# Top-32 selection from pair and quad maxima, and no filler products, in a gated cross-attention and expert block

## The chip, the cores and the metric

One core of one Trainium2 chip runs the whole program as one launch. The metric is device time in microseconds (us). Six runs of the kernel before lie between 1881.35 and 1894.25 us, with a median of 1891.92 us. The engines are named as in the profile: PE multiplies matrices, DVE, ACT and POOL work elementwise, SP issues most transfers. PE writes its products to PSUM, which has eight banks of 512 fp32 values in each of 128 partitions; the other tiles lie in SBUF.

## The reference, cut to what matters

Eight batches of 512 tokens by 256 features pass through two gated blocks. The first is a cross-attention that keeps, in each row of scores, only the 32 largest of 1024, and drives a FiLM modulation around a long convolution, followed by an MLP. The second is a mixture of experts with one of eight experts for each token, beside a shared one. The change is in the attention's selection:

```python
Q = (x_text @ Wq).reshape(Bb, Tt, H, DH)          # 8 x 512 tokens, 4 heads of 32
K = (x_vision @ Wk).reshape(Bb, Gg, H, DH)        # 1024 context rows
scores = jnp.einsum('bthd,bghd->bhtg', Q, K) / np.sqrt(DH)
topv, topi = jax.lax.top_k(scores, K_TOP)         # 32 of 1024 in each row
probs = jax.nn.softmax(topv, axis=-1)
attn = jnp.zeros_like(scores).at[bi, hi, ti, topi].set(probs)
attn_mean = attn.mean(axis=1)                     # over the 4 heads
V = x_vision @ Wv
c_t = jnp.einsum('btg,bgd->btd', attn_mean, V)
```

## The kernel before

**An order by a plan.** The kernel doesn't issue its operations as it writes them. `Plan.note` records each with an engine, an estimated cost and its dependencies, read off the tiles that it reads and writes (lines 100 to 218). `Plan.order` (220 to 307) then plays the program through on those estimates: of the operations that are ready it takes the one that can begin first, and among equals the one with the lowest place `k`; it also grants the buffers of each pool. The result is one fixed order for each engine, and every engine works through its own in order. `Plan.issue` (318 to 326) issues them, so nearly every instruction of the profile bears line 326 and has to be told by its tiles.

**The fillers.** The plan notes how long PE would be idle before each operation (`o.idle`, line 284). Ahead of each PE operation, `issue` calls `busy` (1407), which issues products of `ones16` with itself, 512 columns wide, into a PSUM bank `idle` of its own: one for each 0.22 us of 85% of that idle time, of which at most 12 us are counted (lines 325 and 332). Nobody reads `idle`. In the built program it is 1525 products.

**PSUM.** Its eight banks are two for scores (`ps_sc`), two for accumulators (`ps_ac`), three for all other products (`ps_mm`) and one for the fillers (`ps_id`), lines 389 to 392.

**The work.** Four streams are recorded beside each other: `prepare` (437) loads a batch and makes `kT` and `qT`; `attention` (910) goes through 8 batches x 4 token tiles x 2 pairs of heads, which is 64 pairs; behind it, a batch later, `mixed` (1058) and `after_mix` (1100) do the convolution, the MLP and the shared expert; `routed` (1336) runs 38 blocks of 128 tokens through their expert. Beside the first batch, `setup` (610) makes the convolution's kernel. The last batch's remaining work and 19 of the blocks make a tail without attention, from about 1592 us of the span on.

**One pair of heads** (lines 935 to 986). `scores` has PE make two heads' rows of scores for 128 tokens (`pS`), a pair ahead, and ACT copies them to `sc` (128 x 1024). Then, for each head:

- DVE takes the maximum of the scores' two halves, `mn[:, 0]`, 512 wide (line 943). POOL makes the minimum beside it, exactly, by integers: it adds the halves' bits and subtracts those of the maximum, `mn[:, 1]` (945, 946).
- DVE scans the 512 maxima for the 32 largest: MAX8 gives eight, MATCH_REPLACE strikes them out into `left`, four and three times (948 to 956).
- ACT computes the exponentials `e`, with the largest score subtracted (958).
- DVE scans the 512 minima for their eight largest (965); eight of these and the last eight of the first scan give the row's threshold `th` (967 to 969).
- DVE multiplies `e` by `sc >= th` and sums it (977); ACT counts by signs (979), scales by the sum (982), and POOL adds the heads up in `acc` (984). When a token tile is done, `weighted` (875) transposes `acc` and multiplies it with the context on PE.

The tiles `mn`, `left`, `e`, `top` and `acc` have two buffers each, so those of the next pair wait for this pair's last readers.

**The guard.** At the end the counts must say that exactly 32 scores passed in every row; if not, a general branch computes everything anew (1415 to 1447). The selection above is exact as long as no more than eight of a row's 32 largest are the smaller one of their two halves.

Of the kernel before, what the change touches and what calls it, by code (L numbers as in the profile page):

```python
# [12 lines left out]
F32 = mybir.dt.float32  # L13
# [3 lines left out]
I32 = mybir.dt.int32  # L17
AF = mybir.ActivationFunctionType
ALU = mybir.AluOpType
AX = mybir.AxisListType  # L20
PSUM = bass.MemoryType.PSUM

P = 128
# [20 lines left out]


class Op:
    __slots__ = ("i", "eng", "fn", "cost", "lat", "table", "acc", "succ", "npred", "est", "tiles", "end", "start", "what", "k", "idle")


class Plan:  # L50
# [169 lines left out]
    def order(self):  # L220

        ops = self.ops
        free = {e: 0.0 for e in ("PE", "DVE", "ACT", "POOL", "SP")}
        table = None
        wire = 0.0
        left = {t: len(v[1]) for t, v in self.tiles.items()}
        last = {t: 0.0 for t in self.tiles}
        slots = {}
        for q in self.queues.values():
            slots[id(q)] = [0.0] * q[0]  # L230
        granted = set()
        avail = {e: [] for e in free}
        done = []

        def offer(op):
            op.npred -= 1
            if op.npred == 0:
                avail[op.eng].append(op)

        for op in ops:  # L240
            op.npred += 1 + len(op.tiles)

        def grant(q):
            s = slots[id(q)]
            while s and q[2] < len(q[1]):
                t = q[1][q[2]]
                q[2] += 1
                at = min(s)
                s.remove(at)
                for i in self.tiles[t][1]:  # L250
                    ops[i].est = max(ops[i].est, at)
                    offer(ops[i])

        for q in self.queues.values():
            grant(q)
        for op in ops:
            offer(op)
        total = len(ops)
        while len(done) < total:
            best = None  # L260
            for e, a in avail.items():
                if not a:
                    continue
                t = free[e]
                first = min(max(t, o.est) for o in a)
                c = None
                for o in a:
                    if o.est <= first:
                        k = o.k + (SWITCH if e == "ACT" and o.table not in (None, table) else 0)
                        if c is None or k < c[0]:  # L270
                            c = (k, o)
                o = c[1]
                st = max(t, o.est)
                if best is None or (st, o.k) < best[0]:
                    best = ((st, o.k), o, st)
            assert best is not None, "nothing can begin"
            _, o, st = best
            e = o.eng
            avail[e].remove(o)
            cost = o.cost  # L280
            if e == "ACT" and o.table not in (None, table):
                cost += 1.3
                table = o.table
            o.start, o.idle = st, st - free[e]
            free[e] = o.end = st + cost
            done.append(o)
            if o.lat is not None:
                wire = max(o.end, wire) + (o.lat - 2.9 if o.lat > 2.9 else 0.0)
                fin = max(o.end + o.lat, wire + 2.9)
                o.end = fin  # L290
            else:
                fin = o.end
            for i in o.succ:
                s = ops[i]
                hop = HOP["DMA" if o.lat is not None else e] if (s.eng != e or o.lat is not None) else 0.0
                s.est = max(s.est, fin + hop)
                offer(s)
            for t in o.tiles:
                left[t] -= 1
                last[t] = max(last[t], fin)  # L300
                if left[t] == 0:
                    q = self.tiles[t][0]
                    slots[id(q)].append(last[t] + 0.15)
                    grant(q)
        self.total = max(o.end for o in ops)
        self.free = free
        return done
# [7 lines left out]
                return  # L315
            yield

    def issue(self, tc, busy):

        self.noting = False  # L320
        ET = mybir.EngineType
        with tc.manual_schedule(engines={ET.PE, ET.DVE, ET.Activation, ET.Pool, ET.SP}):
            for o in self.order():
                if o.eng == "PE":
                    busy(int(min(o.idle, FILL_MAX) * FILL / STEP))
                o.fn()  # L326


SLOW = 1.05


FILL_MAX, FILL, STEP = 12.0, 0.85, 0.22
SWITCH = 100
WIRE = 350e3
NPREP = 13
# [5 lines left out]
def bc(ap, axis, n):  # L341

    ap = ap.unsqueeze(axis)
    shape = list(ap.shape)
    shape[axis] = n
    return ap.broadcast_to(shape)
# [3 lines left out]
def tile_kernel(ctx: ExitStack, tc: tile.TileContext, a: dict, out: bass.AP):  # L350
    nc = tc.nc
    x, cx = a["x"], a["ctx_768"]
    B, T, D = x.shape
    G, DV = cx.shape[1:]
    H, DH = 4, 32
    KTOP = 32
    HID = a["L0_xattn_W1"].shape[1]
    NST = a["L0_xattn_A_re"].shape[1]
    NE, _, NI = a["L0_ffn_rt_gate"].shape
# [4 lines left out]

    L = T // 2
    NL, NFFT = L // P, 2 * L
    SCALE = 1.0 / float(np.sqrt(np.float32(DH)))


# [15 lines left out]
    pk = ctx.enter_context(tc.tile_pool(name="pk", bufs=2))  # L385
# [2 lines left out]
    dr = ctx.enter_context(tc.tile_pool(name="dr", bufs=1, space=bass.MemoryType.DRAM))  # L388
    ps_sc = ctx.enter_context(tc.tile_pool(name="ps_sc", bufs=1, space=PSUM))
    ps_ac = ctx.enter_context(tc.tile_pool(name="ps_ac", bufs=2, space=PSUM))  # L390
    ps_mm = ctx.enter_context(tc.tile_pool(name="ps_mm", bufs=3, space=PSUM))
    ps_id = ctx.enter_context(tc.tile_pool(name="ps_id", bufs=1, space=PSUM))
    ctx.enter_context(nc.allow_non_contiguous_dma(reason="small vectors"))

    plan = Plan(nc)
    V, S, GP, TE, SY = (plan.engine(n, e) for n, e in (
        ("DVE", nc.vector), ("ACT", nc.scalar), ("POOL", nc.gpsimd), ("PE", nc.tensor), ("SP", nc.sync)))
# [4 lines left out]
    def bank(name, pool=ps_mm, tag="mm"):  # L402
        return pool.tile([P, 512], F32, tag=tag, name=name)
# [13 lines left out]
    ones16 = const.tile([P, P], BF16, name="ones16")  # L417
# [136 lines left out]
    free = const.tile([P, NE], I32, name="free")  # L554
# [355 lines left out]
    def attention(states):  # L910
# [5 lines left out]
        for k, (b, t, h0) in enumerate(steps):  # L916
            s, sc = states[b], ahead
# [10 lines left out]
            if h0 == 0:  # L928
                acc = pk.tile([P, G], F32, tag="acc", name=f"acc{b}_{t}")
            n = f"{b}_{t}_{h0}"  # L930
# [4 lines left out]
            top = pk.tile([P, 2, KTOP + 8], F32, tag="top", name="top" + n)  # L935
            sm = pk.tile([P, 5, 2], F32, tag="sm", name="sm" + n)
            nm, nb, na, su, ri = (sm[:, k_, :] for k_ in range(5))
            e_, mn = [], []
            for i in range(2):
                m_ = pk.tile([P, 2, G // 2], F32, tag="mn", name=f"mn{n}_{i}")  # L940
                mn.append(m_)
                lo, hi = sc[i][:, : G // 2], sc[i][:, G // 2 :]
                V.tensor_tensor(m_[:, 0], lo, hi, ALU.max)
                mi = m_.bitcast(I32)
                GP.tensor_tensor(mi[:, 1], lo.bitcast(I32), hi.bitcast(I32), ALU.add)
                GP.tensor_tensor(mi[:, 1], mi[:, 1], mi[:, 0], ALU.subtract)
            for i in range(2):
                for r in range(KTOP // 8):
                    t8 = top[:, i, r * 8 : r * 8 + 8]
                    src = mn[i][:, 0] if r == 0 else left  # L950
                    V.max(t8, src)
                    if r == 0:
                        S.activation(nm[:, i : i + 1], t8[:, 0:1], AF.Copy, scale=-SCALE)
                        left = pk.tile([P, G // 2], F32, tag="left", name=f"left{n}_{i}")
                    if r < KTOP // 8 - 1:
                        V.match_replace(left, t8, src, TAKEN)
                e_.append(pk.tile([P, G], F32, tag="e", name=f"e{n}_{i}"))
                S.activation(e_[i], sc[i], AF.Exp, bias=nm[:, i : i + 1], scale=SCALE)
                if i == 0:
                    yield  # L960
                    if behind is not None:
                        behind()
                        behind = None
            for i in range(2):
                V.max(top[:, i, KTOP:], mn[i][:, 1])
            t8 = pk.tile([P, 2, 8], F32, tag="t8", name="t8" + n)
            for i in range(2):
                V.max(t8[:, i, :], top[:, i, KTOP - 8 :])
# [21 lines left out]
    def attention_masked(b, s):  # L990
# [3 lines left out]
        for t in range(NT):  # L994
            acc = pk.tile([P, G], F32, tag="acc", name=f"acc{b}_{t}")
            for h in range(H):
# [14 lines left out]
                for r in range(KTOP // 8):  # L1011
                    src = sc if r == 0 else wk_
                    V.max(top[:, r * 8 : r * 8 + 8], src)
                    if r == 0:
                        GP.tensor_scalar(sm[:, 0:1], top[:, 0:1], -SCALE, None, ALU.mult)
                    V.match_replace(wk_, top[:, r * 8 : r * 8 + 8], src, TAKEN)
# [385 lines left out]
    together(behind(B - 1))  # L1402
    together((routed(B - 1, 0, TAKE[B - 1]), 1))

    idle = bank("idle", ps_id, "id")

    def busy(n):
        for _ in range(n):
            nc.tensor.matmul(idle, ones16, bc(ones16, 1, 4), start=True, stop=True)  # L1409

    plan.issue(tc, busy)


    ok = const.tile([P, 4], F32, name="ok")
# [74 lines left out]
```

## Time and profile before

| | us | share of the span |
|---|---|---|
| median of six runs | 1891.92 | |
| the profiled execution, as timed | 1875.7 | |
| its span, first to last instruction | 1874.0 | 100% |
| PE busy, fillers included | 1712.3 | 91% |
| of it fillers (1525) | 380.7 | 20% |
| DVE busy | 1465.5 | 78% |
| ACT busy | 1173.8 | 63% |
| POOL busy | 1087.4 | 58% |
| mean granted PE clock | 0.955 of full speed | |

Shares of the whole span mix stages with different limits: the first 281 us hold the setup, from 93 to 1592 us most of the attention and the other streams run beside each other, and after 1592 us DVE is busy for 62 of 188 us and PE for 180. Matmuls are pipelined and their ends are modelled: a filler has a mean of 392 ns in the profile, but the next one starts 216 ns after it at full clock. The granted clock is either 1.00 or 0.50 at any moment, and a stretch of time shows the mean.

### The profile page before, as it was taken

Reading aid. Unit: us, or ns where it says so; the run is one execution under the profiler, and the core shown is the slowest. Engines: PE = TensorE matmul, PEld = TensorE weight load, DVE = VectorE, ACT = ScalarE, POOL = GpSimd, SP = SyncE. Lnnn points to the kernel's source line nnn. Section 1 sums busy time; section 2 is a strip of 40 time slices with the busy share of each in tenths; the row PEclk is TensorE's granted clock in tenths of the full one; section 3 lists DMA queues with packets and bytes.
Section 4 is the critical chain, followed back from the end, with each engine's and each line's share of the span. In section 5 each row is a group of like instructions: output and inputs, shape, how many; then the busy total and the mean of one; then the engine's idle time right before and its main releaser. Section 6 shows DMA issues by size and latency. Waiting matters only on the chain. (4 is left out here: it accounts for less than half of the span.)

```text
span 1874.0 us, 24133 instructions
## 1 busy us (share of the span) xinstructions
PE 1712.3 (91%) x7888; PEld 992.3 (53%) x7888; DVE 1465.5 (78%) x2841; ACT 1173.8 (63%) x2020; POOL 1087.4 (58%) x1048
## 2 busy tenths in 40 slices
PE   8598997999989988999889889998999999899996
PEld 4254543445544544565347444654466546547685
DVE  5999988998889888989778989788998999531210
ACT  6577744577757764797468756976697678413221
POOL 6454435665765666577655856585758676532122
PEclk9799998999999988999989999998999999999998
DMA  4000010001100120044003320233013405532594
GB/s 113 0 1 23 21 46 17 1 12 57 57 17 21 48 62 17 23 135 125 18 12 118 99 70 12 73 114 101 12 53 103 115 1 152 169 115 77 191 286 127
DMA packets 101301, 131.88 MB, mean 70 GB/s; under 512 B 9687, under 2 KB 73004, under 8 KB 101166
## 3 DMA queue, kind: packets, MB, share of 16 engines
q1 hardware_dynamic: 93102, 121.05, 20.5%
q0 software_dynamic: 7008, 8.42, 2.6%
q8 instruction: 64, 1.05, 0.2%
q10 hardware_dynamic: 1056, 0.79, 0.1%
q14 instruction: 71, 0.58, 0.1%
HBM read 112.22 MB, written 18.78 MB: 70 GB/s over the span
## 5 line engine op out<-in xcount | busy, mean ns | idle before, releaser
L1409 PE MATMUL idle<-ones 128*128 128x512 bf16 x1525 | 380.7, 392 | 0.0
L326 POOL TENSOR_TENSOR acc<-acc,e 128x1024 f32<-128x1024 f32 x96 | 232.9, 2426 | 136.3 <-ACT e L326 133.6
L326 POOL TENSOR_TENSOR mn<-sc 128x512 int32<-128x512 int32 x128 | 203.9, 1602 | 154.7 <-DVE top L326 97.1
L326 DVE MAX8 top<-left 128x8 f32<-128x512 f32 x384 | 265.4, 691 | 10.4
L1409 PEld LDWEIGHTS <-ones 128*128 128x128 bf16 x1525 | 148.9, 101 | 197.6 <-issue 64.4
L326 DVE SCALAR_TENSOR_TENSOR e<-sc,t,e 128x1024 f32<-128x1024 f32 x128 | 210.1, 1659 | 18.3 <-ACT e L326 18.3
L326 PE MATMUL pS<-kT,qT 32*128 32x512 f32 x512 | 209.9, 664 | 13.8 <-ACT sc L326 13.3
L326 POOL TENSOR_TENSOR mn<-mn 128x512 int32<-128x512 int32 x128 | 180.7, 1423 | 64.8 <-DVE mn L326 61.5
L326 ACT COPY sc<-pS 128x512 f32<-128x512 f32 x256 | 142.8, 584 | 85.0 <-PE pS L326 65.8
L326 DVE MATCH_REPLACE8 left<-top,left 128x512 f32<-128x512 f32 x256 | 172.9, 675 | 0.0
L326 ACT ACT_TABLE_LOAD x130 | 166.8, 1283 | 7.8 <-PE p L326 2.1
L326 DVE MAX8 top<-mn 128x8 f32<-128x512 f32 x256 | 169.1, 678 | 3.0 <-POOL mn L326 2.7
L326 DVE TENSOR_TENSOR mn<-sc 128x512 f32<-128x512 f32 x128 | 149.9, 1195 | 24.1 <-ACT sc L326 24.1
L326 ACT ACTIVATE e<-sc,sm 128x1024 f32<-128x1024 f32 x128 | 146.1, 1148 | 30.6 <-POOL acc L326 27.1
L326 ACT ACTIVATE junk<-sc,sm 128x1024 bf16<-128x1024 f32 x128 | 146.3, 1143 | 1.3
L326 PE MATMUL pu<-aT,cx 128*96 128x128 f32 x1024 | 131.2, 277 | 0.9 <-ACT aT L326 0.9
L326 PEld LDWEIGHTS pu<-aT,cx 128*96 128x96 f32 x1024 | 119.6, 165 | 21.9 <-issue 15.2
L326 POOL DMA_INDIRECT out_dram<-yb,to x38 | 65.8, 1731 | 106.2 <-DMA out_dram<-yb,to 46.0
L326 PE MATMUL pm<-hT,w 128*128 128x512 f32 x256 | 119.1, 598 | 0.3
L326 PE MATMUL am<-w,ga 128*128 128x256 f32 x512 | 117.5, 380 | 2.0 <-ACT ga L326 2.0
L326 ACT ACTIVATE e<-e,sm 128x1024 f32<-128x1024 f32 x96 | 108.7, 1151 | 3.8 <-DVE sm L326 3.7
L326 DVE TENSOR_TENSOR ger<-sgr,pu 128x512 f32<-128x512 f32 x38 | 26.0, 683 | 106.8 <-PE pu L326 92.3
(288 smaller groups left out, 3194.4 us busy)
## 6 DMA issues: line engine op xcount, KB each, us to landing
rt_gate<-in_L_ffn_rt_gate_dram SPq DMA_DIRECT2D x38, 512.0 KB
rt_up<-in_L_ffn_rt_up_dram SPq DMA_DIRECT2D x38, 512.0 KB
rt_down<-in_L_ffn_rt_down_dram SPq DMA_DIRECT2D x38, 512.0 KB
w<-in_L_xattn_W_dram SPq DMA_DIRECT2D x32, 512.0 KB
cx<-in_ctx_dram SPq DMA_DIRECT2D x7, 768.0 KB
xtab<-zt SPq DMA_DIRECT2D x8, 642.5 KB
xb<-xtab SPq DMA_DIRECT2D x38, 128.5 KB
xt<-in_x_dram SPq DMA_DIRECT2D x8, 512.0 KB
```

What stands on the lines that cost most here:

```text
L326: o.fn()
L1409: nc.tensor.matmul(idle, ones16, bc(ones16, 1, 4), start=True, stop=True)
```

## The change

The halves are halved again. With `Q` = 256, DVE takes, after the maximum of halves, the maximum of that maximum's own halves, `hi`, 256 wide, so each element of `hi` is the largest of four scores. The four MAX8 and three MATCH_REPLACE go over these 256. POOL makes the smaller ones for both levels: as before the 512 of the first (add and subtract), and then the 256 of the second (another add and subtract). Both lie side by side in `mn[:, Q:]`, and one scan over the 768 gives their eight largest. The place of the maxima's first quarter, `mn[:, :Q]`, is where the struck-out rows are now written, and the tag `left` holds `hi`. The rest of a pair is as before. The selection is exact as long as no more than eight of a row's 32 largest are not the largest of their four.

The fillers are gone, with the plan's note of idle time and the bank `idle`, and `ps_mm` has four banks.

```diff
     def issue(self, tc, busy):
...
             for o in self.order():
-                if o.eng == "PE":
-                    busy(int(min(o.idle, FILL_MAX) * FILL / STEP))
                 o.fn()
...
-FILL_MAX, FILL, STEP = 12.0, 0.85, 0.22
...
+    Q = G // 4
...
-    ps_mm = ctx.enter_context(tc.tile_pool(name="ps_mm", bufs=3, space=PSUM))
-    ps_id = ctx.enter_context(tc.tile_pool(name="ps_id", bufs=1, space=PSUM))
+    ps_mm = ctx.enter_context(tc.tile_pool(name="ps_mm", bufs=4, space=PSUM))
...
-            e_, mn = [], []
+            e_, mn, hi = [], [], []
             for i in range(2):
-                m_ = pk.tile([P, 2, G // 2], F32, tag="mn", name=f"mn{n}_{i}")
+                m_ = pk.tile([P, G], F32, tag="mn", name=f"mn{n}_{i}")
                 mn.append(m_)
-                lo, hi = sc[i][:, : G // 2], sc[i][:, G // 2 :]
-                V.tensor_tensor(m_[:, 0], lo, hi, ALU.max)
-                mi = m_.bitcast(I32)
-                GP.tensor_tensor(mi[:, 1], lo.bitcast(I32), hi.bitcast(I32), ALU.add)
-                GP.tensor_tensor(mi[:, 1], mi[:, 1], mi[:, 0], ALU.subtract)
+                V.tensor_tensor(m_[:, : 2 * Q], sc[i][:, : 2 * Q], sc[i][:, 2 * Q :], ALU.max)
             for i in range(2):
+                m_ = mn[i]
+                hi.append(pk.tile([P, Q], F32, tag="left", name=f"hi{n}_{i}"))
+                V.tensor_tensor(hi[i], m_[:, :Q], m_[:, Q : 2 * Q], ALU.max)
+                mi, si = m_.bitcast(I32), sc[i].bitcast(I32)
+                GP.tensor_tensor(mi[:, 2 * Q :], si[:, : 2 * Q], si[:, 2 * Q :], ALU.add)
+                GP.tensor_tensor(mi[:, 2 * Q :], mi[:, 2 * Q :], mi[:, : 2 * Q], ALU.subtract)
+                GP.tensor_tensor(mi[:, Q : 2 * Q], mi[:, :Q], mi[:, Q : 2 * Q], ALU.add)
+                GP.tensor_tensor(mi[:, Q : 2 * Q], mi[:, Q : 2 * Q], hi[i].bitcast(I32), ALU.subtract)
+            for i in range(2):
+                left = mn[i][:, :Q]
                 for r in range(KTOP // 8):
                     t8 = top[:, i, r * 8 : r * 8 + 8]
-                    src = mn[i][:, 0] if r == 0 else left
+                    src = hi[i] if r == 0 else left
                     V.max(t8, src)
...
-                        left = pk.tile([P, G // 2], F32, tag="left", name=f"left{n}_{i}")
                     if r < KTOP // 8 - 1:
                         V.match_replace(left, t8, src, TAKEN)
...
             for i in range(2):
-                V.max(top[:, i, KTOP:], mn[i][:, 1])
+                V.max(top[:, i, KTOP:], mn[i][:, Q:])
...
-    idle = bank("idle", ps_id, "id")
-
-    def busy(n):
-        for _ in range(n):
-            nc.tensor.matmul(idle, ones16, bc(ones16, 1, 4), start=True, stop=True)
-
-    plan.issue(tc, busy)
+    plan.issue(tc)
```

More of the change, by code (lines that the diff above doesn't have):

```diff
@@ L46 @@
 class Op:
-    __slots__ = ("i", "eng", "fn", "cost", "lat", "table", "acc", "succ", "npred", "est", "tiles", "end", "start", "what", "k", "idle")
+    __slots__ = ("i", "eng", "fn", "cost", "lat", "table", "acc", "succ", "npred", "est", "tiles", "end", "start", "what", "k")
 class Plan:
@@ L283, in order @@
                 table = o.table
-            o.start, o.idle = st, st - free[e]
+            o.start = st
             free[e] = o.end = st + cost
@@ L316, in ahead, with issue @@
             yield
-    def issue(self, tc, busy):
+    def issue(self, tc):
         self.noting = False
```

## The prediction

> **What bounds the kernel now.** I read the busy times first, then the same by stage, then the groups, then the waits. The stages, in us of the span (columns: stage, length, then busy time and count of PE, PEld, DVE, ACT, POOL, then granted clock, DMA share, GB/s):
>
> ```profile
> 0.00:93.00 93.00, 63.59 (x252) 28.74 (x252) 70.17 (x127) 54.16 (x102) 48.23 (x68) 0.87 0.22 57
> 93.00:281.00 188.00, 177.53 (x1216) 91.67 (x1217) 175.70 (x255) 129.03 (x205) 88.74 (x58) 0.97 0.07 23
> 281.00:562.00 281.00, 255.81 (x998) 129.20 (x997) 245.93 (x481) 176.98 (x311) 180.37 (x146) 0.96 0.09 27
> 562.00:937.00 375.00, 351.30 (x1403) 194.46 (x1405) 324.98 (x657) 263.16 (x457) 246.76 (x244) 0.95 0.19 56
> 937.00:1311.00 374.00, 341.23 (x1465) 202.18 (x1464) 315.39 (x624) 264.68 (x454) 240.09 (x235) 0.94 0.26 75
> 1311.00:1592.00 281.00, 268.26 (x1196) 161.72 (x1194) 261.90 (x526) 214.21 (x362) 196.89 (x188) 0.98 0.25 72
> 1592.00:1780.00 188.00, 180.15 (x833) 117.65 (x832) 62.36 (x164) 54.62 (x97) 62.00 (x88) 0.98 0.42 138
> ```
>
> From 93 to 1592 us, while the 64 pairs of heads are selected, DVE is busy 175.70 + 245.93 + 324.98 + 315.39 + 261.90 = 1323.9 of 1499 us, 88%; POOL 952.9 us, 64%. PE looks busier, but its fillers are in that number. So DVE paces the selection with 175 us idle, and PE paces the tail after 1592 us. The groups that the change touches (busy us, mean ns of one, idle before):
>
> ```profile
> L1409 PE MATMUL idle<-ones 128*128 128x512 bf16 x1525 | 380.7, 392 | 0.0
> L326 DVE MAX8 top<-left 128x8 f32<-128x512 f32 x384 | 265.4, 691 | 10.4
> L326 DVE SCALAR_TENSOR_TENSOR e<-sc,t,e 128x1024 f32<-128x1024 f32 x128 | 210.1, 1659 | 18.3 <-ACT e L326 18.3
> L326 DVE MAX8 top<-mn 128x8 f32<-128x512 f32 x256 | 169.1, 678 | 3.0 <-POOL mn L326 2.7
> L326 DVE TENSOR_TENSOR mn<-sc 128x512 f32<-128x512 f32 x128 | 149.9, 1195 | 24.1 <-ACT sc L326 24.1
> L326 POOL TENSOR_TENSOR yf<-yf,t 128x256 f32<-128x256 f32 x32 | 27.5, 880 | 0.0
> L326 DVE TENSOR_TENSOR ger<-sgr,pu 128x512 f32<-128x512 f32 x38 | 26.0, 683 | 106.8 <-PE pu L326 92.3 <-PE pxb L326 12.6 <-ACT sgr L326 2.0
> L326 DVE TENSOR_TENSOR xr<-xr,pfo 128x256 f32<-128x256 f32 x64 | 25.8, 418 | 12.5 <-ACT xr L326 4.1 <-DMA xtab<-zt 3.8 <-PE pfo L326 2.1
> L326 DVE MAX8 t<-top 128x8 f32<-128x16 f32 x128 | 18.6, 167 | 0.1
> ```
>
> See the two 512-wide TENSOR_TENSORs: 1195 ns with both operands in SBUF, 683 with one in PSUM. One by one in the trace, the first kind takes about 689 ns in 71 of 128 cases and 1839 on average in the other 57, and those lie almost wholly beside a POOL operation: the two engines hold each other up. Last, three waits (us in total, times, longest):
>
> ```profile
> POOL acc L326 <- ACT e L326: 133.6, 29, 10.3
> POOL mn L326 <- DVE top L326: 97.1, 27, 14.5
> DVE xm L326 <- PE pfi L326: 54.9, 20, 8.6
> ```
>
> POOL is often ahead and waits. In before nobody needs its minima before the last scan.
>
> **The shorter scans.** MAX8 costs (678 - 167) / (512 - 16) = 1.03 ns an element, so 256 elements save 0.264 us. Per head, four MAX8 and three MATCH_REPLACE (675 ns at 512; same slope taken) shrink: 7 x 0.264 = 1.85 us; the scan of the rest grows from 512 to 768: 0.264 back. Over 128 heads: -203 us.
>
> **The added maximum of quarters (DVE, 256 wide, two SBUF operands).** Before has 418 ns for this size with one operand in PSUM; the held-up half-maximum is 0.51 over its PSUM twin. I take 0.93 us x 128 = +119 us; bounds 0.418 (54 us) and 0.418 plus one whole 512-wide POOL operation, 1.27 (216 us). I take the middle because POOL is by construction at work on the same pair just then.
>
> **More holding up.** The half-maximum loses 0.51, the 1024-wide selection 1659 - 1219 (its PSUM neighbour) = 0.44: 122 us over 128 heads. POOL gets 2 x 0.87 us per head more (the 880 ns row): 223 us, so 64% becomes some 78% and the 122 us grow by 23%: +28 us. Bounds 0 and 60. DVE net: -203 + 119 + 28 = **-56 us**. POOL's 223 us themselves lie beside DVE and are not added.
>
> **The new wait.** The first MATCH_REPLACE of a head now writes into the first quarter of `mn`, which POOL must have read: its 512-wide add and subtract and the 256-wide add come first. Behind it in DVE's queue stand the scans of both heads, the thresholds, and with them ACT's and POOL's work of the pair. In the timeline of the 64 pairs POOL's subtract of the first head ends 5.60 us on average (median 4.53, one in ten over 11.35) after DVE began the pair; plus 0.87 is 6.5. DVE's own work until then: two half-maxima, two quarter-maxima, two MAX8: 2 x (1.195 + 0.93 + 0.41) = 5.1. That is 1.4 us short. The built order of the changed program, priced with these rows, says the same: between the two points POOL has 9.6 us queued on average, other operations included, DVE 8.1. So some 1.45 x 64 = 93 us; I count two thirds, **+60 us**, since part falls on the 175 us that DVE idles anyway. Bounds: 0 (POOL begins early, as it often could) and 192 (only the pairs where POOL is late, 3.0 us a pair).
>
> **The fillers go.** Of their runs, those followed at once by a real product may have held it up: 86 us before 281 us, 90 from there to 1592, 22 after. Against that stands the clock:
>
> ```profile
> 516.00:519.20 3.20, 1.13 (x11) 0.91 (x9) 3.10 (x6) 0.37 (x1) 0.00 (x0) 1.00 0.16 32
> 519.20:522.60 3.40, 0.62 (x3) 0.63 (x4) 2.69 (x6) 0.00 (x0) 3.06 (x2) 0.51 0.61 201
> ```
>
> PE was busy for a third of a step, and the next step ran at half clock, where the filler's spacing is 427 ns for 216. Cutting the record of the clock into its 3.41 us steps, all 19 full-clock steps with PE under 47% busy are followed by a half-clock one, and a drop lasts 1.7 steps on average. With the fillers struck out of the trace, low steps between 281 and 1592 us rise from 20 to 64: 44 x 1.7 x 3.41 / 2 = 128 us of PE time lost, against 90 at most won. A third of either counts, since DVE paces this stage and PE ends under two thirds of its idle time: 43 - 30 = **+13 us** (bounds -90, +128). In the tail PE is the path: 5 more low steps, +14, less 22: **-8**. At the start the products before the first selection at 32 us sum to some 7 us at full clock; **+5** of it (0 to 10). Between 32 and 281 us DVE covers PE, so 86 us won and 50 low steps count nothing; without that cover it is within those bounds.
>
> The Trainium skill, in TensorE: Matmul & The Clock Gate, "What's actually happening", puts the return to half clock after an idle window of about 3.4 us. The trace is stricter: the step above was a third busy. Wholly idle steps in that stage would rise from 3 to 22, so by the rule the 128 us would be an estimated 55, the share on the path 18 and the sum 25 us lower.
>
> **The fourth bank.** PE's list of waits shows none that a product bank ends; 0, bounds -20 and +10. DMA work is the same, except in place.
>
> **Sum:** -56 + 60 + 13 - 8 + 5 = +14 us. The profiled execution took 1875.7 us (span 1874.0), so 1890; the six runs have their median at 1891.92, 0.87% above, and the forecast at that level is **1906 us**.
>
> **Rivals.**
> (1) *POOL keeps ahead*, and the new wait vanishes. It decides if the first 256-wide add ends within 5.1 us of the pair's start in most pairs; half of the subtracts end within 4.53 already, which speaks for it, the acc waits of up to 10.3 us in POOL's queue against. Then -56 + 10 = -46, and with the quarter-maximum at its floor -111: 1765 to 1830 and, at the median's level, 1780 to 1846. The faster side, with what lies between it and my forecast.
> (2) *The clock bounds it*: PE has so little to spare after 562 us that all 128 us and none of the 90 count. It decides once real products fill most half-clock steps. +14 - 13 + 128 = +129: 2005, at the median's level 2022.
> (3) *POOL bounds it*: per pair its work becomes (952.9 + 223) / 64 = 18.4 us, and if it keeps before's idle 547 / 64 = 8.5, a pair takes 26.9 instead of 23.4: +224 us, some 2115; half of that is likelier.
> (4) *The selection fails its own test*, and the general branch runs: that needs a row with over 8 of its 32 largest outside the quarter-maxima. Counted from the given inputs, the worst of 16,384 rows has 7. Under 1%.
>
> **How the numbers follow.** Within 1886 to 1950, the forecast's terms as taken or somewhat worse: 0.42 (0.09 of it within 0.3% of before, which is about what a measurement can tell from no change; 0.33 slower). Rival 1 and what lies between: 0.36. Rivals 2 and 3, in whole or half: 0.22. So faster 0.36, same 0.09, slower 0.55. Both signs hold much, so the forecast's own range is 1886 to 1950, and the one for 8 in 10 is 1815 to 2015.
>
> **What would show it.** DVE's MAX8 at 256 near 0.41 us; the 256-wide maximum near 0.9; a new group of waits of DVE's first MATCH_REPLACE on POOL `mn` near 60 to 90 us; the clock near 0.85 instead of 0.955; DVE's busy time near 1410. Wrong if that wait stays under 20 us, or if DVE idles on PE's products instead.

## The result, and the profile after

The changed kernel takes 1891.69 us (median of 35 runs, 1884.53 to 1894.54), the kernel before 1883.16 us (median of 77): a ratio of **1.0038, 95% interval 1.0024 to 1.0051**. It is slower by 7.2 us of 1883. The six runs that the forecast was read against had their median 0.5% above that of the 77. Of the twelve runs of experiment e2 below, three (1893 to 1897 us, at a clock of 0.83) count as slow and are left out of its ratio; with them its mean ratio would be 0.9989, so every size below that rests on e2 could be some 7 us off. The profiled execution has a span of 1889.2 us against 1874.0.

The same stages as before (stage, length, busy time and count of PE, PEld, DVE, ACT, POOL, clock, DMA share, GB/s):

```profile
93.00:281.00 188.00, 105.57 (x729) 64.90 (x729) 167.28 (x257) 127.35 (x199) 108.03 (x75) 0.61 0.07 22
281.00:562.00 281.00, 219.41 (x681) 114.39 (x682) 221.06 (x481) 166.00 (x296) 209.62 (x188) 0.78 0.08 27
562.00:937.00 375.00, 327.01 (x1204) 185.25 (x1203) 306.56 (x679) 262.45 (x456) 296.32 (x301) 0.87 0.18 56
937.00:1311.00 374.00, 327.82 (x1342) 197.65 (x1341) 302.98 (x683) 269.57 (x467) 294.26 (x308) 0.90 0.25 75
1311.00:1592.00 281.00, 257.10 (x980) 148.62 (x978) 234.97 (x535) 194.91 (x335) 227.72 (x222) 0.89 0.19 57
1592.00:1780.00 188.00, 162.52 (x705) 108.05 (x703) 69.53 (x191) 70.43 (x120) 82.16 (x108) 0.93 0.43 143
```

From 93 to 1592 us DVE's busy time fell from 1323.9 to 1232.9 us and POOL's rose from 952.9 to 1136.0. Yet the last maximum of halves begins at 1598.5 us, where it began at 1588.2: DVE has 91 us less to do in that stretch (78.5 us less in the whole span) and is no sooner done. The clock fell in every stage, to a mean of 0.837. The groups (busy us, mean ns, idle before):

```profile
L323 DVE SCALAR_TENSOR_TENSOR e<-sc,t,e 128x1024 f32<-128x1024 f32 x128 | 204.4, 1612 | 18.1 <-ACT e L323 16.7
...
L323 DVE MAX8 top<-mn 128x8 f32<-128x256 f32 x384 | 163.9, 427 | 12.2
...
L323 DVE TENSOR_TENSOR mn<-sc 128x512 f32<-128x512 f32 x128 | 138.8, 1107 | 7.0 <-ACT sc L323 6.9
L323 DVE TENSOR_TENSOR hi<-mn 128x256 f32<-128x256 f32 x128 | 133.0, 1065 | 0.6
...
L323 DVE MAX8 top<-mn 128x8 f32<-128x768 f32 x128 | 119.2, 944 | 7.0 <-POOL mn L323 6.9
L323 POOL TENSOR_TENSOR mn<-mn 128x256 int32<-128x256 int32 x128 | 111.8, 874 | 12.6 <-DVE hi L323 8.1
...
L323 POOL TENSOR_TENSOR mn<-mn,hi 128x256 int32<-128x256 int32 x128 | 105.7, 826 | 8.1
...
L323 DVE MATCH_REPLACE8 mn<-top,mn 128x256 f32<-128x256 f32 x256 | 104.6, 408 | 0.0
...
L323 DVE MATCH_REPLACE8 mn<-top,hi 128x256 f32<-128x256 f32 x128 | 52.2, 408 | 0.0
...
L323 DVE MAX8 top<-hi 128x8 f32<-128x256 f32 x128 | 49.7, 412 | 0.3
```

A scan of 256 takes 0.41 to 0.43 us for 0.68 to 0.69. The 256-wide maximum takes 1065 ns, two and a half times the 418 ns of that size with an operand in PSUM. And the waits:

```profile
PEld pS L323 <- ACT sc L323: 131.1, 83, 16.0
...
POOL mn L323 <- DVE top L323: 72.7, 22, 14.6
...
DVE mn L323 <- POOL mn L323: 57.8, 26, 6.6
DVE xm L323 <- PE pfi L323: 56.7, 18, 14.9
...
POOL acc L323 <- ACT e L323: 43.8, 18, 8.6
```

The line to see is `DVE mn <- POOL mn`: the new wait of the MATCH_REPLACE that writes into `mn`. POOL's own waits for `acc` fell from 133.6 to 43.8 us: it is less often early.

### The profile page after: what moved, and what is told of

The parts are those of the page before. It is cut to its first block, busy times and chain, and to the rows that moved or that the text cites. A ratio compares the mean times of both kernels' runs of the same rounds, so it can differ in the third digit from the quotient of the medians.

```text
span 1889.2 us, 21516 instructions
## 1 busy us (share of the span) xinstructions
PE 1531.3 (81%) x6363; PEld 918.9 (49%) x6363; DVE 1387.0 (73%) x2969; ACT 1163.5 (62%) x2015; POOL 1300.6 (69%) x1304
## 5 line engine op out<-in xcount | busy, mean ns | idle before, releaser
L323 POOL TENSOR_TENSOR mn<-mn 128x256 int32<-128x256 int32 (+1 forms) x256 | 291.4, 1144 | 48.5 <-DVE mn L323 32.8
L323 PE MATMUL pS<-kT,qT 32*128 32x512 f32 x512 | 254.9, 768 | 71.6 <-ACT sc L323 71.3
L323 DVE MAX8 top<-mn 128x8 f32<-128x256 f32 (+1 forms) x512 | 276.6, 556 | 19.2 <-POOL mn L323 6.9
L323 POOL TENSOR_TENSOR mn<-sc 128x512 int32<-128x512 int32 x128 | 188.1, 1474 | 122.7 <-DVE top L323 72.7
L323 POOL TENSOR_TENSOR acc<-acc,e 128x1024 f32<-128x1024 f32 x96 | 230.8, 2404 | 59.1 <-ACT e L323 43.8
L323 DVE SCALAR_TENSOR_TENSOR e<-sc,t,e 128x1024 f32<-128x1024 f32 x128 | 204.4, 1612 | 18.1 <-ACT e L323 16.7
L323 PEld LDWEIGHTS pS<-kT,qT 32*128 32x128 f32 x512 | 72.4, 213 | 179.7 <-ACT sc L323 131.1
L323 PE MATMUL pm<-hT,w 128*128 128x512 f32 x256 | 143.7, 698 | 15.0 <-ACT hT L323 13.0
L323 DVE TENSOR_TENSOR mn<-sc 128x512 f32<-128x512 f32 x128 | 138.8, 1107 | 7.0 <-ACT sc L323 6.9
L323 DVE TENSOR_TENSOR hi<-mn 128x256 f32<-128x256 f32 x128 | 133.0, 1065 | 0.6
L323 PEld LDWEIGHTS am<-w,ga 128*128 128x128 f32 x512 | 103.6, 206 | 48.4 <-ACT ga L323 23.2
L323 POOL TENSOR_TENSOR mn<-mn,hi 128x256 int32<-128x256 int32 x128 | 105.7, 826 | 8.1
L323 POOL TENSOR_TENSOR yf<-yf,t 128x512 f32<-128x512 f32 (+1 forms) x80 | 94.7, 1209 | 16.5 <-DVE t L323 14.5
```

## The experiments

Ratios are to the kernel before on the same chip, with 95% intervals. Ratios of two of them are worked out here, with both half-widths added as squares. "Pairs" is the selection of before, "quads" the changed one. A plan made for other operations, costs or banks gives another order of all queues, and that alone can move the time. So I compared programs that share one order where I could. The built programs of before and e3 do, instruction by instruction, fillers aside; so do e1 and e9, e2 and e11, e3 and e8, the changed kernel with e10, e12 and e17, and e15 with e18 (in e10 and e18 without the operations left out). All other comparisons are between two orders.

**e1, quads with fillers.** The new selection put into the kernel before; `ps_mm` keeps three banks, fillers stay.

> The new selection alone: quads as in the changed kernel, fillers and three product banks as in before. Theory 1 (the selection gains some 20 us, as DVE's 78 us less work lose 58 to the new wait for POOL, and the missing fillers lose some 35): ratio to before 0.985 to 0.993, granted clock near 0.95. Rival 2 (the missing fillers cost nothing and the selection itself loses what was lost, since POOL has become the bound): 1.002 to 1.010. Rival 3 (neither part does anything by itself, the small loss is one of order): within 0.003 of 1.

1.0140 (1.0099 to 1.0182): 26 us slower. Theory 1 falls. Rival 2's sign holds, beyond its range of 1.002 to 1.010; but this is another order than before's, so it is not shown that the work alone costs that.

**e2, pairs without fillers, four banks.** The other part alone.

```diff
-                    busy(int(min(o.idle, FILL_MAX) * FILL / STEP))
...
-    ps_mm = ctx.enter_context(tc.tile_pool(name="ps_mm", bufs=3, space=PSUM))
-    ps_id = ctx.enter_context(tc.tile_pool(name="ps_id", bufs=1, space=PSUM))
+    ps_mm = ctx.enter_context(tc.tile_pool(name="ps_mm", bufs=4, space=PSUM))
```

> The other part alone: no fillers and four product banks, the selection in two parts as in before. Theory 1: the slower clock costs some 35 us, ratio 1.014 to 1.022, granted clock 0.83 to 0.87. Rival 2: 0.99 to 1.003 at the same low clock, since DVE paces the stage and covers PE. Rival 3: within 0.003 of 1.

0.9952 (0.9918 to 0.9985), at a clock of 0.844. By this ratio the part is a gain, and theory 1 is wrong here too. The number is within rival 2's range; e3 and e8 show that it doesn't come about in rival 2's way.

**e3, the same with three banks** (`bufs=3`).

> As the run before, but with the three product banks of before; one bank stays unused, so that the difference between the two is the fourth bank alone. Theory 1 took the bank as worth nothing: within 0.003 of that run. Rival 4 (the fourth bank pays for part of what the clock costs): slower than that run by 5 to 20 us.

1.0145 (1.0103 to 1.0187). Its order is before's, so the missing fillers cost 1.45%, 27 us, and rival 2 (the slower clock costs nothing) falls. Its profile has the clock of 0.836 beside 0.955:

```profile
core 0: 1917.5 us, clock 0.836
```

From e3 to e2 the fourth bank is worth 1.0145 to 0.9952, a ratio of 0.981 (0.976 to 0.986): 36 us, more than the 5 to 20 of rival 4, where theory 1 had nothing.

**e8, the order of three banks on four.** e2's kernel, whose plan believes in three.

```diff
-                        q = self.queues.setdefault(t.tag, [meta.bufs, [], 0])
+                        q = self.queues.setdefault(t.tag, [3 if t.tag.startswith("mm_") else meta.bufs, [], 0])
```

> The second experiment's kernel (no fillers, four banks) with its order made as if there were three: order of the third experiment, banks of the second. Theory D (the fourth bank is worth its 36 us on the chip, because PE or its readers wait less): near the second, ratio 0.992 to 1.002. Theory E (it is the plan that puts operations in a better order with four): near the third, ratio 1.010 to 1.016.

1.0138 (1.0092 to 1.0184): e3's time. In this order the fourth bank by itself is worth nothing on the chip (0.9993, 0.993 to 1.005): the 36 us come with the order that the plan makes when it knows of four banks. Theory E.

**e9, quads without fillers, three banks** (the changed kernel with `bufs=3`).

> The changed kernel with three product banks instead of four: its order is that of the first experiment (quads with fillers), instruction by instruction, without the fillers. Before and the third experiment (pairs, three banks) also share one order, and there the fillers were worth 1.45%. Theory F (fillers are worth some 25 us at a fixed order, whatever the selection): ratio to before 1.024 to 1.034, and the fourth bank's better order then hides it in the changed kernel. Theory G (with quads DVE has room and the fillers are worth little): 1.012 to 1.020.

1.0287 (1.0243 to 1.0331). Beside e1, which has its order, the fillers are worth 1.45% again: theory F. Beside the changed kernel, the fourth bank with the order made for it is worth 2.4%.

**e4, a tile of its own for the struck-out rows.**

```diff
-                left = mn[i][:, :Q]
+                left = pk.tile([P, Q], F32, tag="lf", name=f"left{n}_{i}")
```

> The changed kernel, but the struck-out rows go into a tile of their own and not over the first quarter of mn, so DVE's first MATCH_REPLACE no longer waits for POOL; the last scan still does. Theory 1: the 57.8 us of that wait go; a part comes back as waits of the last scan and of others, so 20 to 45 us faster than the changed kernel, ratio to before 0.98 to 0.993. Rival 2 (POOL is the bound, the wait only moves to the last scan): within 6 us of the changed kernel, and DVE's waits for POOL mn stay near 60 us in all.

1.0026 (0.9994 to 1.0058): the changed kernel's time. The 57.8 us wait is gone, and others have grown in its place, DVE's on ACT's exponentials (16.7 before) and on the minima for the last scan (6.9):

```profile
DVE e L323 <- ACT e L323: 35.7, 16, 6.5
DVE top L323 <- POOL mn L323: 27.8, 19, 4.5
```

The time is rival 2's, the waits are not: DVE's for POOL `mn` are 27.8 us, less than half of the 60 it asked for. And the plan had made another order for the new tile, so the run couldn't tell; e17 does.

**e5, without POOL's second minima.** The two 256-wide POOL lines are left out.

> The changed kernel without POOL's 256-wide add and subtract (a part of the computation left out: the smaller ones of the second level are not made, the last scan reads maxima in their place, and the final test of the counts always passes). DVE's work is that of the changed kernel, POOL's that of before. Theory A (POOL's added work, 217 us, gives DVE's gain back): 20 to 40 us faster than the changed kernel, ratio to before 0.982 to 0.993. Theory B (DVE's work no longer sets the pace, whatever POOL does): within 6 us of the changed kernel, ratio 1.000 to 1.007.

0.9886 (0.9846 to 0.9926), 28 us faster than the changed kernel: theory A, if it isn't the order.

**e10, the same in the changed kernel's own order.**

```diff
                 GP.tensor_tensor(mi[:, Q : 2 * Q], mi[:, :Q], mi[:, Q : 2 * Q], ALU.add)
+                plan.ops[-1].fn = lambda: None
                 GP.tensor_tensor(mi[:, Q : 2 * Q], mi[:, Q : 2 * Q], hi[i].bitcast(I32), ALU.subtract)
+                plan.ops[-1].fn = lambda: None
```

> The changed kernel in its own exact order; POOL's two 256-wide operations per head are planned but not issued (left out: the smaller ones of the second level; the final test of the counts always passes). The fifth experiment's 28 us could be order or work. If it is POOL's work (theory A): 20 to 35 us faster than the changed kernel, ratio 0.985 to 0.994. If it was order (theory E again): within 8 us of the changed kernel.

0.9842 (0.9801 to 0.9884): 37 us faster than the changed kernel at one and the same order (0.9805, 0.976 to 0.985), a little more than expected. In its profile the new wait is down from 57.8 us; what is left is for POOL's 512-wide subtract, which reads the same quarter:

```profile
DVE mn L323 <- POOL mn L323: 17.9, 9, 4.0
```

**e17, that wait alone taken away at the same order.** The plan sees the changed kernel; what is issued writes to another tile.

```diff
+                own = pk.tile([P, Q], F32, tag="lf", name=f"left{n}_{i}")
...
                     V.max(t8, src)
+                    if r:
+                        plan.ops[-1].fn = partial(nc.vector.max, t8, own)
...
                         V.match_replace(left, t8, src, TAKEN)
+                        plan.ops[-1].fn = partial(nc.vector.match_replace, own, t8, own if r else src, TAKEN)
```

> The changed kernel in its own exact order, but the struck-out rows really go into a tile of their own, so DVE's first MATCH_REPLACE doesn't wait for POOL (in the fourth experiment the plan knew of the new tile and made another order). If that wait is what POOL's added work costs: 25 to 40 us faster than the changed kernel, ratio to before 0.982 to 0.991. If POOL's lateness only moves to the last scan, which still needs the minima: within 12 us of the changed kernel, ratio 0.997 to 1.004, with DVE's waits of top for POOL mn grown to 25 us or more.

0.9904 (0.9871 to 0.9937): 25 us faster than the changed kernel (0.9866, 0.983 to 0.990), and faster than before. So about two thirds of the price of POOL's work is this wait (25 of 37 us; the two intervals overlap a little); a part of the rest shows as the last scan's wait, 6.9 us in the changed kernel:

```profile
DVE top L323 <- POOL mn L323: 21.5, 17, 2.9
```

**e6, the minima made twice.** e2 with the same POOL load and none of DVE's savings.

```diff
                 GP.tensor_tensor(mi[:, 1], mi[:, 1], mi[:, 0], ALU.subtract)
+                GP.tensor_tensor(mi[:, 1, :Q], lo[:, :Q].bitcast(I32), hi[:, :Q].bitcast(I32), ALU.add)
+                GP.tensor_tensor(mi[:, 1, :Q], mi[:, 1, :Q], mi[:, 0, :Q], ALU.subtract)
```

> No fillers, four banks and the selection in two parts, as in the second experiment (ratio 0.9952), but POOL makes half of each row's minima a second time: the same 256-wide add and subtract per head that the change adds, with DVE's work as in before. Theory A: 15 to 35 us slower than the second experiment, ratio 1.003 to 1.014. Theory B: within 6 us of it, ratio 0.992 to 0.999.

0.9982 (0.9959 to 1.0006): 6 us slower than e2 (1.0030, 0.999 to 1.007), between the theories and not clear of either. Its order is not e2's either, so the 6 us are not the price of the work alone. Here DVE reads the minima only in the last scan, behind all the long ones, and hardly waits for them:

```profile
DVE top L323 <- POOL mn L323: 2.5, 6, 0.6
```

That fits a load that is dear only where its result is read early, but this run doesn't show it; e17 does, at one order.

**e7, the plan's clock.** The changed kernel with `SLOW = 1.2` for 1.05.

> The changed kernel with the plan's factor on PE's costs at 1.2 instead of 1.05; no instruction is added or taken away, the order alone changes. Theory C (the order was made for the clock of 0.955 that the fillers held, and at 0.837 PE runs late against it): 10 to 25 us faster than the changed kernel, ratio 0.990 to 0.999. Otherwise within 10 us either way, which then tells what a change of order alone is worth here.

1.0323 (1.0272 to 1.0375): 54 us slower than the changed kernel, with the same instructions. Theory C falls, and an order alone can be worth more than the whole change.

**e11, fillers into the next product's bank, pairs.** e2 with fillers ahead of the first product of a bank:

```diff
+                    t = getattr(o.out, "tensor", o.out)
+                    if t.name not in begun:
+                        begun.add(t.name)
+                        busy(t, int(min(o.idle, FILL_MAX) * FILL / STEP))
...
+            nc.tensor.matmul(t[:], ones16, bc(ones16, 1, 4), start=True, stop=True)
```

> The second experiment's order (pairs, four banks) with fillers that need no bank: each goes into the very bank that the next new product will overwrite, and only ahead of the first product of a bank. Theory F: the clock returns to 0.93 or more and some 20 us are gained, ratio 0.978 to 0.990, faster than both kernels. Otherwise (the fillers block PE's queue as much as they help): 0.992 to 1.003.

1.0130 (1.0081 to 1.0179): 34 us slower than e2, although the clock is back at 0.932. These fillers (line 1409 there) have to wait until the bank is free, and then stand before the very product that its readers wait for. ACT's wait for scores is 152.6 us, in e2 (the last line) 85.8:

```profile
ACT sc L330 <- PE pS L330: 152.6, 72, 12.3
...
PE pS L1409 <- ACT sc L330: 76.1, 34, 9.7
...
ACT sc L323 <- PE pS L323: 85.8, 72, 7.7
```

**e12, the same with quads.**

> The changed kernel, in its own order, with the same fillers in the next product's bank. Theory F: some 20 us faster than the changed kernel, ratio 0.988 to 0.998. Theory G: within 6 us of the changed kernel. Beside the run before it, this also gives the selection's own price with four banks and fillers; by theory A the quads are then slower than the pairs by 0.5 to 1.5%.

1.0180 (1.0138 to 1.0222), 1.4% slower than the changed kernel (with pairs it was 1.8%). Theories F and G both miss. These fillers differ from before's in their bank, in their places and in the order around them; which of these turns a gain into a loss is not separated. Quads are 0.5% slower than e11, inside the two intervals.

**e13 to e16, four programs in other orders** (`SLOW = 1.1`, no fillers).

> The second experiment (pairs, no fillers, four banks) with the plan's factor on PE's costs at 1.10 instead of 1.05: another order, the same work. Theory E1 (a plan that knows of four banks is better as a rule): 15 to 40 us faster than the next run. Theory E2 (the four-bank order at 1.05 was a lucky one of many, which differ by 1 to 3% whatever changes them): no such rule, ratio anywhere from 0.99 to 1.03.

> The third experiment (pairs, no fillers, three banks) at the factor 1.10. Theory E1: 1.010 to 1.025 and 15 to 40 us slower than the run before it. Theory E2: as likely faster as slower than that run.

> The changed kernel at the factor 1.10. Theory E1: 15 to 40 us faster than the next run. If the quads themselves cost what they cost at 1.05 (0.9% with four banks, 1.4% with three): that much slower than the pairs of the first run of this call; under theory E2 the two differ in either direction.

> Quads, no fillers, three banks, at the factor 1.10. Theory E1: 1.015 to 1.040, the slowest of the four. Theory E2: anywhere in 0.99 to 1.03.

| no fillers | plan 1.05 | plan 1.10 |
|---|---|---|
| pairs, 4 banks | 0.9952 (0.9918 to 0.9985) | **0.9844 (0.9809 to 0.9879)** |
| pairs, 3 banks | 1.0145 (1.0103 to 1.0187) | 1.0165 (1.0123 to 1.0207) |
| quads, 4 banks | 1.0038 (1.0024 to 1.0051) | 1.0284 (1.0248 to 1.0320) |
| quads, 3 banks | 1.0287 (1.0243 to 1.0331) | 1.0294 (1.0258 to 1.0330) |

With pairs the four-bank plan is better again, by 3.2%, 60 us, more than theory E1's 15 to 40; with quads its 2.4% is gone (0.1%). So neither theory holds whole: a rule for pairs in two orders, none for quads. The quads are slower than the pairs in all four places, by 0.9, 1.4, 4.5 and 1.3%. e13 is the fastest complete kernel of the study, 1850.62 us, and beats both that were compared.

**e18, e15 without POOL's second minima, in its order** (the edit of e10).

> The quads with four banks at the factor 1.10 (ratio 1.0284), in that exact order, with POOL's 256-wide operations planned but not issued (left out: the smaller ones of the second level; the final test of the counts always passes). At 1.05 the same step was worth 37 us. Theory A, POOL's work at any order: 25 to 45 us faster than that run, ratio 1.004 to 1.015. If that order loses its 2.5% elsewhere: the same gain, and still slower than 1.004; if its loss is waiting for POOL: 60 us or more, ratio under 0.996.

0.9968 (0.9941 to 0.9996): 59 us faster than e15, more than the 37 us at 1.05 and at the edge of the last case. POOL's price is there in both orders, and its size depends on the order.

## Why the prediction was wrong, step by step

The sign, the +14 us on a profiled execution (15.2 by the two spans) and most durations came close. In measured times, though, the change is 7.2 us or 0.38%, half of the 0.75% forecast, and that it came so near is luck: three errors cancel. From before over e3 and e2 to the changed kernel, the change is made of +27 us for the missing fillers (10 forecast), -36 us for the order with four banks (0 forecast) and +16 us for the quads with their own order (1.0038 / 0.9952 = 1.0086, 1.005 to 1.012; 4 forecast), together +7. Only the first is a price at one order. Over e1 and e9 the same change is +26 for the quads, +28 for the fillers and -47 for the fourth bank with its order: the signs agree, but two of the sizes depend on the path.

- *The fourth bank*, "0, bounds -20 and +10", is **the step that failed**. I looked for waits that end with a product bank, found none, and priced the bank at nothing. That was right for the chip in one order (e8: 0.9993) and wrong for this kernel: the bank count is also an input of the plan, and the order made with four banks brought 36 us with pairs. I had the built order of the changed program at hand, and read it for the new wait alone.
- *The fillers*, +13 - 8 + 5 = +10 us, cost 27. The mean clock was foreseen well, 0.837 for 0.85, and so was the number of half-clock steps between 281 and 1592 us: 34 + 44 x 1.7 = 109, and the changed kernel has 104 of 385. But that too is two errors that cancel: its steps with PE under 47% busy are 35 there and not 64, and its 36 drops last 2.9 steps each and not 1.7 (in e3, before's own order without fillers: 51 such steps, 31 drops of 3.5). The 27 us are the net of the slower clock and of what PE gains without fillers. The runs don't give the two apart, so whether the third of the loss that I put on the path was too little, or the 30 us that the fillers were to have cost by holding PE up too much, stays open. That a product followed a filler at once does not show that it was held up.
- *The shorter scans*: -203 us forecast; MAX8 went from 434.5 to 332.8 us, MATCH_REPLACE from 259.4 to 156.8: -204.
- *The 256-wide maximum*: 0.93 us taken, 1.065 measured, 133 us for 119.
- *More holding up*: +28 us taken. The half-maximum fell from 149.9 to 138.8 us and the selection from 210.1 to 204.4: -17. The trace shows what a held-up operation waits for: the end of the POOL operation that is running when it starts (last section). Half-maxima over 0.76 us rose from 55 to 66 of 128, near the +23% taken from POOL's share, but their mean fell from 1.88 to 1.51 us; selections over 1.35 us went from 66 to 62. POOL's share of the time is no measure of what holding up costs.
- *DVE net*: -56 taken, -78.5 in its whole busy time (1465.5 to 1387.0).
- *The new wait*: 60 us taken, 57.8 in the list, though both times behind it were too early. The first 256-wide add ended 9.4 us after the pair's start on average, for 6.5, and DVE's first MATCH_REPLACE began 10.9 us after it, waits included, for 5.1; the built order's 9.6 and 8.1 were nearer. As the price at a fixed order it is 25 us (e17), and all of POOL's added work 37 (e10). What I missed is the other side: DVE's 78 us less work seem to bring little. e10 has them, with POOL's work as before, and is 1.1% under e2, 21 us, though in another order. That the 64 pairs are bound by waits from engine to engine as well as by DVE's work would explain it; no run shows it.
- *Rival 1* decided on POOL being early in most pairs; it was not: the first 256-wide add ended within 5.1 us of the pair's start in 14 of 64 pairs. *Rival 2* needed half-clock steps full of real products on the path; the missing fillers cost 27 us in all at one order, not 128. *Rival 3*, POOL as the only bound, is refuted by e17, where POOL has all of its work and the kernel is 25 us faster.

How the clock behaved: in the profile after, all 24 full-clock steps with PE under 47% busy were followed by half clock, and only 5 of those 24 were wholly idle. The Trainium skill, in TensorE: Matmul & The Clock Gate, "What's actually happening", ties the return to an idle window. The trace is stricter here too. But a step under 47% is not the only way down: 26 of the 50 drops in that profile follow full-clock steps with PE about half busy or more, some of them busy throughout, and in e3 33 of the 36 low steps were followed by half clock, not all.

What stays open: why the plan's order with four banks is so much better for pairs. It was not traced to single waits, and for the quads it is there at one factor and not at the other; there, the bank and its order were not tried apart either. Nor is it known how far the quads' remaining price at plan 1.10 is order.

## What to carry to other kernels

Where a planner decides the order, a change is two changes: the work, and the order made for it. Price the first at a fixed order (plan an operation and don't issue it, or issue another in its place), and vary a constant of the plan to see how far order alone scatters; here that was nearly 3%, over seven times the effect. When work moves to a slower engine, ask first how soon its result is needed: with the same POOL operations in the same order, 25 us went when DVE no longer wrote over a tile that POOL still had to read (e17). A buffer written over is such an early reader.

## What the runs showed of the hardware

In this kernel half clock costs less than it seems: at one order, from the kernel before to e3, the mean clock fell from 0.955 to 0.836, 12.5%, and the time at half clock rose from 172 to 629 us of the span, yet the kernel took only 1.45% longer. A clock of 0.932 came with a slower kernel (e11) than one of 0.844 (e2).

A DVE operation on two SBUF tiles that starts while POOL is in an elementwise operation on wide tiles can be held until that operation ends. In the changed kernel 80 of the 128 256-wide maxima took over 0.6 us, where the least is 0.403; POOL was at work at the start of all 80, and 79 ended 0.27 to 0.30 us after the end of a POOL operation. With the 512-wide maxima it is the same in both kernels: those over 0.76 us (55 before, 66 after; least 0.657) all started beside a running POOL operation and ended 0.53 to 0.57 us after one's end. The POOL operation can be one on other tiles (`acc`, `yf`). So a held-up operation pays what is left of the POOL operation, and now and then of the next one too: the one running at the start was the one whose end let it go in 76 of the 80, 49 of the 55 and 65 of the 66 cases.
